# A two-layer graph attention kernel: fourteen edge tiles a layer fetched row by row, node rows kept in SBUF, a first stage with fixed row buffers

## The chip, the cores and the metric

The kernel runs on one core of a Trainium2 chip, as one program in one launch. The metric is the device time of one execution in microseconds (us), without a profiler. Before the change the median of three runs is 2140.39 us (2140.09 to 2140.89). One further execution was profiled, and all rows of profiles below come from such an execution.

The engines are named as in the profile: PE (TensorE; PEld is its weight load), DVE (VectorE), ACT (ScalarE), POOL (GpSimd) and SP (SyncE, which only issues transfers).

## What is computed

6250 nodes have 768 features each; 100,000 edges (src, dst) are sorted by dst, and each node has an edge to itself besides. Cut to what matters:

```python
h = maximum(layernorm(x), 0)                 # 6250 x 768
for W, heads in ((W1, 4), (W2, 1)):          # two layers
    h = h @ W                                # 256 features
    e = leaky_relu(alpha_s[src] + alpha_d[dst])
    w = exp(e - max over the edges of dst)
    h = sum over edges of dst (w * h[src]) / sum of w
    h = relu(h + b)
out = x + relu(h @ Wm1 + bm1) @ Wm2 + bm2
```

alpha_s and alpha_d are products of a node's 256 features with a vector for each head. The costly part is h[src]: 100,000 rows of about 1 KB a layer, at places that only the data tells.

## The kernel before, in words

Nodes are cut into 49 tiles of 128 (NT), edges into 784 tiles of 128 (NET). Tiles 2 to 783 hold edges, so a layer has 782. Four edge tiles are a group (196 groups, NG), two are a pair (392), and 16 belong to one node tile.

**First stage** (L236 to L375), one pass for each node tile. SP loads x and its transpose (L180, L245). DVE takes the moments (L251, L253), PE spreads the mean over partitions (L264), DVE subtracts it (L270), ACT applies relu (L272), and PE multiplies by W1, 12 matrix instructions (L281). ACT writes the result into `row`, one of 5 rotating buffers (L288), whose ones and scores POOL fills (L287, L306). POOL multiplies by the score vectors and halves the sum twice (L296, L299), DVE adds up the rest (L305). SP stores the row into `table1` in DRAM (L309). From tile 14 on one piece of `edge_places` (L186) is put between tiles: integer arithmetic on the edges' numbers by DVE, and their loads.

**The two edge stages** (`layer_edges`, L433). For every edge tile POOL issues one indirect transfer, which fetches 128 rows of the table at the places that a column of `src_i` holds (`gather`, L448, L456). It is issued 8 groups ahead (AHEAD), into 10 buffers. Six pairs a layer, `singles` (L122: pairs 71, 135, ... 391), are not fetched by POOL. SP fetches their 256 rows each, one transfer for a row (`fetch_singles`, L460). It loads 32 numbers of rows into registers (L465), and for each row computes the place and issues the transfer (L470). The generator is resumed once after each pair (L623, L636) and issues 4 rows, so that a pair takes 64 pairs' time and is there 7 pairs ahead of its use.

For each pair (`pair`, L532) ACT makes two exponentials of the sources' scores (L542, L544), DVE combines them with those of the destinations (L547) and scales the rows (layer 1, L559) or a one-hot matrix (layer 2, L554), and PE sums over edges by a one-hot product (L570). A group's sums run on in `acc` (L585). When a node tile is complete, `Node1.steps` adds the node's own row, divides, multiplies by W2 and stores into `table2` (L683 to L707). `Node2.steps` runs the two dense layers and stores the output (L775 to L817). The own row of a node comes from the table in DRAM: `prefetch` loads it from SP (L675, L760), and DVE uses it in `ahead` (L680) or `steps` (L778).

The order on each engine is the order in which the program is written (`manual_schedule`), so a waiting instruction holds up all behind it on its engine. SP has one queue, and on it stand the rows of `singles`, the own rows, the masks (L431, L493), destinations (L425), x and outputs. Every SP transfer counts on one of eight semaphores in turn, and waits for the one eight before it.

Of the kernel before, what the change touches and what calls it, by code (L numbers as in the profile page):

```python
# [11 lines left out]
BF16 = mybir.dt.bfloat16  # L12
I32 = mybir.dt.int32
AF = mybir.ActivationFunctionType
ALU = mybir.AluOpType
AX = mybir.AxisListType

P = 128
N = 6250
# [18 lines left out]
AHEAD = 8  # L38
SPAN = 8
ROWS = 4  # L40
REGS = 32
PAD_DST = 1 << 20
# [3 lines left out]
CH = P * TPC  # L46
NCH = EP // CH


@with_exitstack  # L50
def kernel(
# [68 lines left out]
    dcol = const.tile([P, NET], F32, name="dcol")  # L120

    singles = range(2 * TPG * SPAN + 7, NET // 2, 2 * TPG * SPAN)  # L122
    single_i = const.tile([1, len(singles), 2 * P], I32, name="single_i")
    dmod_d = dram.tile([NCH, CH], BF16, name="dmod_d")
# [58 lines left out]
    def heads_row(row):  # L183
        return row[:, :RW[1]].rearrange("p (h c) -> p h c", h=4)

    def edge_places(ones):  # L186

        dst_i = ones.tile([P, NET], I32, name="dst_i")
        dri = ones.tile([NCH, CH], I32, name="dri")
        for to, of in ((dst_i, dst_cols), (dri, dst_rows), (src_i, src_cols)):  # L190
            nc.sync.dma_start(to, of)
            yield
            yield
        nc.sync.dma_start(single_i, src_rows[singles[0]::singles.step].unsqueeze(0))
        yield
        for layer in bT:
            with nc.allow_non_contiguous_dma(reason="256 numbers"):
                nc.sync.dma_start(bT[layer], {1: b1, 2: b2}[layer].rearrange("(k p) -> p k", p=P))
            yield
        b = ones.tile([P, OUT_DIM // P], F32, name="b")  # L200
        with nc.allow_non_contiguous_dma(reason="768 numbers"):
            nc.sync.dma_start(b, bm2.rearrange("(p k) -> p k", p=P))
        yield

        drm = ones.tile([NCH, CH], BF16, name="drm")
        for d, n, w, to, f in ((dst_i, P, NET, dcol, dst_f), (dri, NCH, CH, drm, None)):
            m = ones.tile([n, w], I32, name=f"m{n}")
            nc.vector.tensor_scalar(m, d, P - 1, None, ALU.bitwise_and)
            yield
            if f is None:  # L210
                f = ones.tile([n, w], F32, name=f"f{n}")
            nc.vector.tensor_copy(f, d)
            yield
            far = ones.tile([n, w], F32, name=f"far{n}")
            nc.vector.tensor_scalar(far, f, float(N), 256.0, ALU.is_ge, ALU.mult)
            yield
            nc.vector.tensor_add(to, far, m)
            yield
        nc.sync.dma_start(dmod_d, drm)
        bp = ones.tile([P, 3, OUT_DIM // P], BF16, name="bp")  # L220
        rest = ones.tile([P, 2, OUT_DIM // P], F32, name="brest")
        in_parts(nc.vector, [bp[:, k] for k in range(3)], b, rest[:, 0], rest[:, 1])
        yield
        with nc.allow_non_contiguous_dma(reason="768 numbers"):
            nc.sync.dma_start(bm2_d.rearrange("s (p k) -> p s k", p=P), bp)
# [5 lines left out]
    rowsp = edges_stack.enter_context(tc.tile_pool(name="rows", bufs=3))  # L231
    maskp = edges_stack.enter_context(tc.tile_pool(name="masks", bufs=6))
    bm2_d = dram.tile([3, OUT_DIM], BF16, name="bm2_d")
    mask_d = dram.tile([NU * P, 8 * P], BF16, name="mask_d")
    edges_stack.enter_context(tc.manual_schedule())
    with tc.tile_pool(name="w1p", bufs=1) as wp, tc.tile_pool(name="x1", bufs=6) as xp, \  # L236
# [30 lines left out]
        def centre(i):  # L267
            m_ps, rstd = means.pop(i)
            c = wk.tile([P, KI, P], F32, name="cent")
            nc.vector.tensor_sub(c, xTs.pop(i), m_ps.unsqueeze(1).to_broadcast([P, KI, P]))  # L270
            r = wk.tile([P, KI, P], F32, name="r")
            nc.scalar.activation(r, c, AF.Relu)  # L272
            rs[i] = r, rstd
# [10 lines left out]
        def keep1(i, h_ps, rstd):  # L284
            row = wk.tile([P, TW[1]], F32, name="row", bufs=5)
            h = heads_row(row)[:, :, :HID // 4]
            nc.gpsimd.memset(heads_row(row)[:, :, HID // 4:], 1.0)  # L287
            nc.scalar.activation(h, h_ps.rearrange("p (h c) -> p h c", h=4), AF.Copy, scale=rstd)  # L288

            ha = wk.tile([P, 8, HID // 4], F32, name="ha")  # L290
            four = ha.rearrange("p (k h) c -> p k h c", k=2)
            of = h.unsqueeze(1).to_broadcast([P, 2, 4, HID // 4])
            if i == NT - 1:
                nc.vector.tensor_tensor(four, of, a1b, ALU.mult)
            else:
                nc.gpsimd.tensor_tensor(four, of, a1b, ALU.mult)  # L296
                for n in (HID // 8, HID // 16):
                    hb = wk.tile([P, 8, n], F32, name=f"ha{n}", bufs=4)
                    nc.gpsimd.tensor_tensor(hb, ha[:, :, :n], ha[:, :, n:], ALU.add)  # L299
                    ha = hb  # L300
            rows[i] = row, ha

        def scores1(i):
            row, ha = rows[i]
            nc.vector.tensor_reduce(sd[1][:, i], ha, AX.X, ALU.add)  # L305
            (nc.gpsimd if i < NT - 1 else nc.vector).tensor_copy(row[:, RW[1]:], sd[1][:, i, :4])  # L306

        def store1(i):
            nc.sync.dma_start(table[1][i * P:(i + 1) * P], rows.pop(i)[0])  # L309


        rows = {}
        warm_ps = ps.tile([P, 4 * P], F32, name="warm_ps", tag="o", bufs=3)
# [119 lines left out]
    def layer_edges(layer, H, node, pre, matched):  # L433
# [4 lines left out]
        with tc.tile_pool(name=f"eg{layer}", bufs=4) as eg, \  # L438
# [9 lines left out]
            def gather(g):  # L448
# [3 lines left out]
                for t in tiles(g):  # L452
                    k = TPG * g + t
                    if k // 2 in singles:
                        continue
                    nc.gpsimd.indirect_dma_start(  # L456
                        out=G[g][:, t], out_offset=None, in_=table[layer],
                        in_offset=bass.IndirectOffsetOnAxis(ap=src_i[:, k:k + 1], axis=0))

            def fetch_singles():  # L460

                for j, k in enumerate(singles):
                    single[k] = eg.tile([P, 2, TW[layer]], F32, name="single", bufs=2)
                    for r in range(0, 2 * P, REGS):
                        _, rows = nc.values_load_multi_w_load_instructions(  # L465
                            single_i[:, j, r:r + REGS], engines=(mybir.EngineType.SP,), min_val=0,
                            max_val=N - 1, skip_runtime_bounds_check_because="sources are nodes")
                        for i in range(REGS):
                            t, at = divmod(r + i, P)
                            nc.sync.dma_start(single[k][at:at + 1, t], table[layer][ds(rows[i], 1)])  # L470
                            if i % ROWS == ROWS - 1:
                                yield

            one_by_one = fetch_singles()


# [141 lines left out]
            for g in range(NG):  # L618
# [3 lines left out]
                advance(g)  # L622
                next(one_by_one, None)  # L623
                make_hot(g + 1)
# [10 lines left out]
                advance(g)  # L635
                next(one_by_one, None)  # L636
                if j == 3:
# [29 lines left out]
    with tc.tile_pool(name="w2p", bufs=1) as wp, tc.tile_pool(name="wk2", bufs=2) as wk:  # L667
        w2 = []

        class Node1:  # L670
            rows, mine = {}, {}

            def prefetch(self, t):
                self.rows[t] = wk.tile([P, RW[1]], F32, name="row1", bufs=3)
                nc.sync.dma_start(self.rows[t], table[1][t * P:(t + 1) * P, :RW[1]])  # L675

            def ahead(self, t):
                C = HID // 4
                self.mine[t] = wk.tile([P, 4, C + 1], F32, name="mine")
                nc.vector.tensor_mul(self.mine[t], heads_row(self.rows.pop(t)),  # L680
                                     pre1.own[:, t].unsqueeze(2).to_broadcast([P, 4, C + 1]))

            def steps(self, t, sum_):  # L683
# [17 lines left out]
                for _ in range(4):  # L701
                    yield 1
                row = wk.tile([P, TW[2]], F32, name="row2")
                nc.scalar.activation(row[:, :HID + 1], h_ps[:, :HID + 1], AF.Copy)
# [10 lines left out]
    with tc.tile_pool(name="wmp", bufs=1) as wp, tc.tile_pool(name="x3", bufs=4) as xp, \  # L715
# [39 lines left out]
        class Node2:  # L755
            rows, xs = {}, {}

            def prefetch(self, t):
                self.rows[t] = wk.tile([P, RW[2]], F32, name="row3", bufs=3)
                nc.sync.dma_start(self.rows[t], table[2][t * P:(t + 1) * P])  # L760
                for i in (t - 1, t) if t == NT - 1 else (t - 1,) if t else ():
# [13 lines left out]
            def steps(self, t, sum_):  # L775
                n = min(P, N - t * P)
                all_ = wk.tile([P, RW[2]], F32, name="all_")
                nc.vector.scalar_tensor_tensor(all_, self.rows.pop(t), pre2.own[:, t], sum_,  # L778
                                               ALU.mult, ALU.add)
# [340 lines left out]
```

## Time and profile before

| | us |
|---|---|
| median of three runs, without the profiler | 2140.39 |
| the profiled execution | 3330.35 |
| its span, first to last instruction | 3328.5 |
| first gather of layer 1 starts at | 160.26 |
| last gather of layer 1 starts at | 1817.05 |
| first gather of layer 2 starts at | 1881.18 |
| last gather of layer 2 starts at | 3266.36 |

In a group's row the columns are: line, engine, operation, tiles, count, then busy time and mean ns of one, then the engine's idle time before it and what ended it. "SPq" is SP's queue and "issue" is time in which the engine waited for nothing that the profile shows. Note the first two rows of the table: the profiled execution is 1190 us longer than one without the profiler.

### The profile page before, as it was taken

The numbers are of one execution on the slowest core, as the hardware profiler recorded it, in microseconds if no ns is written. First come the engines' busy times: TensorE is split into PE (matmuls) and PEld (weight loads), VectorE is DVE, ScalarE is ACT, GpSimd is POOL, SyncE is SP. The second block draws the span as 40 slices with busy tenths as digits, with TensorE's granted clock in tenths as the row PEclk, the third lists the DMA queues.
The fourth block names the chain that finished last, engine by engine and source line by source line (L and its number), as shares of the span: only waits on it lengthen the run. The fifth ranks groups of instructions, "written<-read, shape, count | busy, mean of one in ns | idle before, by whom it ended". The sixth has DMA issues, their size and how long they took to land. (4 is left out here: it accounts for less than half of the span.)

```text
span 3328.5 us, 35557 instructions
## 1 busy us (share of the span) xinstructions
PE 1634.9 (49%) x6633; PEld 1105.0 (33%) x6634; DVE 1401.5 (42%) x4321; ACT 554.9 (17%) x2549; POOL 1589.3 (48%) x1791
## 2 busy tenths in 40 slices
PE   9824434434344344344344535555555555564556
PEld 7612223222222222232222323433344333343334
DVE  7824434434344344344343524434443334343344
ACT  4501111111111111111111201111111111111112
POOL 7864434434434344344344255545554555554551
PEclk9956766767767667667776757777777767777768
DMA  9743333333333333333333334444444444444443
GB/s 343 256 132 103 102 98 100 103 95 101 99 98 101 95 104 103 95 100 100 99 101 92 92 96 121 125 121 130 122 121 122 126 124 127 122 126 117 118 128 99
DMA packets 176298, 395.60 MB, mean 119 GB/s; under 512 B 39757, under 2 KB 69674, under 8 KB 176066
## 3 DMA queue, kind: packets, MB, share of 16 engines
q0 software_dynamic: 73920, 205.89, 23.2%
q1 hardware_dynamic: 100908, 186.02, 16.7%
q10 hardware_dynamic: 1238, 1.32, 0.1%
q14 instruction: 175, 1.43, 0.1%
q8 instruction: 57, 0.93, 0.1%
HBM read 334.89 MB, written 58.19 MB: 118 GB/s over the span
## 5 line engine op out<-in xcount | busy, mean ns | idle before, releaser
L456 POOL DMA_INDIRECT G<-table,src_i x1540 | 1461.9, 949 | 1648.9 <-issue 1444.6
L570 PE MATMUL o_ps<-hw,hot 128*128 128x260 f32 x1564 | 610.3, 530 | 970.7 <-DVE hw L559 826.6
L570 PEld LDWEIGHTS o_ps<-hw,hot 128*128 128x128 f32 x1564 | 355.9, 252 | 1221.9 <-DVE hw L559 968.1
L570 PE MATMUL o_ps<-G,hw 128*128 128x258 f32 x1540 | 496.0, 468 | 56.6 <-issue 24.5
L547 DVE TENSOR_TENSOR e_ps<-e,e_ps 128x8 f32<-128x8 f32 (+1 forms) x782 | 127.9, 164 | 863.3 <-ACT e L544 400.3
L596 ACT ACTIVATE sum<-acc 32x260 f32<-32x260 f32 (+1 forms) x384 | 159.9, 416 | 1870.2 <-DVE acc L585 1237.0
L570 PEld LDWEIGHTS o_ps<-G,hw 128*128 128x128 f32 x1540 | 346.4, 237 | 155.8 <-issue 39.1
L680 DVE TENSOR_TENSOR mine<-row,own 128x260 f32<-128x260 f32 x49 | 21.0, 429 | 760.0 <-DMA row<-table 760.0
L554 DVE TENSOR_SCALAR hw<-iota_ps,dcol,w 128x128 f32<-128x128 f32 x782 | 284.8, 405 | 20.4 <-issue 3.1
L520 PE MATMUL e_ps<-win,mask 128*128 128x12 bf16 (+1 forms) x1564 | 62.8, 169 | 467.0 <-DMA mask<-mask_d 457.9
L559 DVE TENSOR_TENSOR hw<-G,e_ps 128x520 f32<-128x520 f32 x385 | 267.8, 696 | 21.9 <-issue 4.0
L807 PE MATMUL y_ps<-wm,mT 128*128 128x384 f32 x392 | 195.2, 631 | 96.4 <-ACT mT L798 91.2
L520 PEld LDWEIGHTS <-mask 128*128 128x128 bf16 x1564 | 60.4, 102 | 484.5 <-DMA mask<-mask_d 462.9
L585 DVE SCALAR_TENSOR_TENSOR acc<-acc,keep,o_ps 128x260 f32<-128x260 f32 (+1 forms) x388 | 184.5, 475 | 25.9 <-PE o_ps L570 15.7
L542 ACT ACTIVATE e<-G 128x8 f32<-128x8 f32 (+1 forms) x770 | 153.1, 199 | 80.4 <-issue 43.4
L544 ACT ACTIVATE e<-G 128x8 f32<-128x8 f32 (+1 forms) x770 | 147.9, 192 | 0.0
L281 PE MATMUL h_ps<-w,r 128*128 128x256 f32 x588 | 134.7, 382 | 6.6 <-ACT r L272 6.6
L807 PEld LDWEIGHTS y_ps<-wm,mT 128*128 128x128 f32 x392 | 82.6, 234 | 157.1 <-ACT mT L798 99.4
L502 DVE TENSOR_TENSOR hot<-iota_ps,dcol 128x512 f32<-128x512 f32 (+1 forms) x196 | 133.6, 682 | 0.0
L663 ACT ACTIVATE rT<-tp,bT 128x128 f32<-128x128 f32 x196 | 60.2, 357 | 381.2 <-PE tp L657 367.0
L281 PEld LDWEIGHTS h_ps<-w,r 128*128 128x128 f32 x588 | 107.9, 190 | 26.9 <-ACT r L272 11.5
L811 DVE TENSOR_TENSOR y<-y_ps,xt 128x384 f32<-128x384 f32 (+1 forms) x98 | 54.1, 552 | 91.6 <-PE y_ps L807 45.1
(403 smaller groups left out, 1165.6 us busy)
## 6 DMA issues: line engine op xcount, KB each, us to landing
xt<-in_x SPq DMA_DIRECT2D x96, 384.0 KB
drow<-dmod_d SPq DMA_DIRECT2D x49, 512.0 KB
mask_d<-mask SPq DMA_DIRECT2D x98, 256.0 KB
mask<-mask_d SPq DMA_DIRECT2D x98, 256.0 KB
G<-table,src_i POOLq DMA_INDIRECT x1540
single<-table SPq DMA_DIRECT2D x1536, 1.0 KB
single<-table SPq DMA_DIRECT2D x1536, 1.0 KB
xTt<-in_xT SPq DMA_DIRECT2D x49, 384.0 KB
```

Of the source, the lines that this page charges most:

```text
L281: nc.tensor.matmul(h_ps, r[:, k], w1[:, k], start=(k == 0), stop=(k == KI - 1))
L456: nc.gpsimd.indirect_dma_start(out=G[g][:, t], out_offset=None, in_=table[layer], in_offset=bass.IndirectOffsetOnAxis(ap=src_i[:, k:k + 1] ...
L502: nc.vector.tensor_tensor(hot[g][:, T[0]:T[0] + n], iota_ps.unsqueeze(1).to_broadcast([P, n, P]), dcol[:, k:k + n].unsqueeze(2).to_broadca ...
L542: nc.scalar.activation(e1, sc, AF.Exp)
L544: nc.scalar.activation(e2, sc, AF.Exp, scale=SLOPE)
L547: nc.vector.tensor_mul(v, e2, rho)
L554: nc.vector.tensor_scalar(hw[:, t], iota_ps, dcol[:, k:k + 1], w[:, t], ALU.is_equal, ALU.mult)
L559: nc.vector.tensor_mul(hw, Gp[:, :, :RW[1]].rearrange("p t (h c) -> p t h c", h=H), w.unsqueeze(3).to_broadcast([P, 2, H, C + 1]))
L570: nc.tensor.matmul(o_ps[g], l, r[:, :RW[layer]], start=(k == tiles(g)[0]), stop=(k == TPG - 1))
L585: nc.vector.scalar_tensor_tensor(acc, run[0], ones_c if last else keep[:, k:k + 1], o_ps.pop(g), ALU.mult, ALU.add)
L596: nc.scalar.activation(done[t][r], acc[r], AF.Copy)
L807: nc.tensor.matmul(y_ps, mT[:, j], wm2[:, j, s * half:(s + 1) * half], start=False, stop=(j == KH - 1))
```

## The change

Four things are changed.

1. **Pairs by rows.** Seven pairs a layer instead of six (59, 111, ... 371), five rows after each pair instead of four. A pair takes 52 pairs' time, and again is there 7 pairs ahead.
2. **Places in bytes.** In the first stage DVE multiplies the numbers of the sources by the row's size in bytes, for each layer (L231), and SP stores them into `place_d`. SP loads 256 of them for a pair, one pair ahead, and the number in the register is the place itself, the table being read as bytes.
3. **Own rows kept.** The 49 rows that the first stage makes stay in SBUF (`kept`, 1056 bytes a partition each). Layer 1 reads them there, `Node1.steps` writes its result over the same buffers and stores it to `table2` as before, and `Node2.steps` reads it there. The 98 loads at L675 and L760 are gone.
4. **First stage.** With a buffer for each tile the five rotating ones are gone. POOL writes the ones of all 49 ahead of the stage. The scores are copied into the row by ACT instead of POOL. In `edge_places` six of DVE's eight wide instructions go; ACT makes three wide conversions to float in their place. `cent`, `r`, `ha` have 2 buffers instead of 3, `ha32` 2 instead of 4.

```diff
+BY_ROWS = {"sync": (5, 32)}
+SLACK = 7
...
+    steps_ = -(-PAIR // rows_)
+    SINGLE[name_] = range(steps_ + SLACK, NET // 2, steps_)
...
-    singles = range(2 * TPG * SPAN + 7, NET // 2, 2 * TPG * SPAN)
...
-        for d, n, w, to, f in ((dst_i, P, NET, dcol, dst_f), (dri, NCH, CH, drm, None)):
-            m = ones.tile([n, w], I32, name=f"m{n}")
-            nc.vector.tensor_scalar(m, d, P - 1, None, ALU.bitwise_and)
-            nc.vector.tensor_copy(f, d)
-            nc.vector.tensor_scalar(far, f, float(N), 256.0, ALU.is_ge, ALU.mult)
-            nc.vector.tensor_add(to, far, m)
+        nc.scalar.activation(dst_f, dst_i, AF.Copy)
+        for d, to in ((dst_i, dcol), (dri, drm)):
+            nc.vector.tensor_scalar(d, d, PAD_DST | P - 1, None, ALU.bitwise_and)
+            nc.scalar.activation(to, d, AF.Copy)
...
+        for layer in (1, 2):
+            nc.vector.tensor_scalar(place, some, 4 * TW[layer], None, ALU.mult)
+            nc.sync.dma_start(place_d[layer], place)
...
+    kept = [keptp.tile([P, TW[1]], F32, name=f"kept{t}") for t in range(NT)]
...
-            row = wk.tile([P, TW[1]], F32, name="row", bufs=5)
-            nc.gpsimd.memset(heads_row(row)[:, :, HID // 4:], 1.0)
+            row = kept[i]
...
-            (nc.gpsimd if i < NT - 1 else nc.vector).tensor_copy(row[:, RW[1]:], sd[1][:, i, :4])
+            nc.scalar.activation(kept[i][:, RW[1]:], sd[1][:, i, :4], AF.Copy)
...
-                            nc.sync.dma_start(single[k][at:at + 1, t], table[layer][ds(rows[i], 1)])
-                            if i % ROWS == ROWS - 1:
+                of = table[layer].bitcast(U8).rearrange("n w -> (n w)").unsqueeze(0)
+                            eng.dma_start(to[p:p + 1, t * W:(t + 1) * W], of[:, ds(at[i], W)])
+                            if (r + i) % step == step - 1:
                                 yield
...
-                self.rows[t] = wk.tile([P, RW[1]], F32, name="row1", bufs=3)
-                nc.sync.dma_start(self.rows[t], table[1][t * P:(t + 1) * P, :RW[1]])
+                pass
...
-                row = wk.tile([P, TW[2]], F32, name="row2")
+                row = kept[t][:, :TW[2]]
...
-                self.rows[t] = wk.tile([P, RW[2]], F32, name="row3", bufs=3)
-                nc.sync.dma_start(self.rows[t], table[2][t * P:(t + 1) * P])
...
-                nc.vector.scalar_tensor_tensor(all_, self.rows.pop(t), pre2.own[:, t], sum_,
+                nc.vector.scalar_tensor_tensor(all_, kept[t][:, :RW[2]], pre2.own[:, t], sum_,
```

## The prediction, made before the result was known

> **What bounds the kernel now.** The first thing to read is a contradiction: the profiled execution took 3330.35 us (span 3328.5, and 1.85 around it), the median without the profiler is 2140.39. So 1190 us of this profile are not in the number to be predicted, and I first had to find which. I read, in this order, the groups by line of POOL, the list of waits, SP's timeline, then PE's timeline of the first stage.
>
> ```profile
> span 3328.5 us, 35557 instructions
> ...
> L456 POOL DMA_INDIRECT G<-table,src_i x1540 | 1461.9, 949 | 1648.9 <-issue 1444.6
> ```
>
> POOL has the most work in the edge stages, but waits longer than it works. Its timeline shows that this is two things:
>
> ```profile
> 1716.01 0.95 POOL L456 DMA_INDIRECT G<-table,src_i  x1 [0.30 <-issue]
> 1717.26 0.95 POOL L456 DMA_INDIRECT G<-table,src_i  x1 [0.30 <-issue]
> 1733.72 0.95 POOL L456 DMA_INDIRECT G<-table,src_i  x1 [15.51 <-issue]
> 1734.97 0.95 POOL L456 DMA_INDIRECT G<-table,src_i  x1 [0.30 <-issue]
> ```
>
> A gather costs POOL 1.25 us from start to start, 0.95 busy and a fixed 0.30; and about once for each node tile POOL stands for 15 us. Who makes it stand is in the waits:
>
> ```profile
> POOL G L456 <- issue: 1444.6, 1361, 17.4
> ...
> DVE mine L680 <- DMA row<-table: 760.0, 46, 17.9
> PEld L520 <- DMA mask<-mask_d: 462.9, 48, 22.3
> ```
>
> DVE waits once for each node tile of layer 1 for a row that SP has yet to request, PE in layer 2 for a mask; POOL then runs out of free buffers. SP's timeline tells why SP is late:
>
> ```profile
> 1130.64 3.50 SPq L470 DMA_DIRECT2D single<-table  x8
> 1134.24 0.36 SPq L493 DMA_DIRECT2D mask_d<-mask  x1
> 1134.79 21.74 SPq L470 DMA_DIRECT2D single<-table  x16
> ```
>
> The same instructions take 0.44 us a row in one line and 1.36 in the next. In the quick stretches a row takes 0.413 us (at 1016.04, four rows in 1.47 us: the last transfer's own 0.23 taken off, 1.24 over 3). I take the slow stretches to be made by the profiler, because without it there is no room for them:
>
> start to first gather 160.3; 770 gathers of 1.25 us, 962.5; layer change 14.8 (landing of the last gather 2.0, as from 1885.87 to its first use at 1887.87, less the fixed 0.3; from the last pairs' scores at 1868.05 to the next layer's first gather at 1881.18, 13.1); 962.5 again; end 21.8 (1.7 as before, one pair 1.1, and 19.0 from the last pair's scores at 3309.48 to the end); around the span 1.85. Sum 2123.8. The row buffer's memset at L705 stretches a gather by 0.12 us in each of 49 node tiles (1775.30 to 1776.67 is 1.37), 5.9 more: 2129.7. The median is 10.7 above that, 0.5%. So without the profiler POOL is in step for nearly all of the two edge stages: gathers times 1.25 us set the time, and SP, though busy, keeps up: per layer 1536 rows x 0.413 + 48 register loads x 2.14 (L465) + 49 x 1.85 for its other transfers = 828 us of POOL's 962.
>
> **The change, part by part** (against 2140.4; a difference under 0.2%, 4.3 us, cannot be told from none).
>
> 1. *Two more edge tiles a layer by rows.* POOL issues 768 gathers a layer instead of 770: 4 x 1.25 = **5.0 us** less, all on the path. SP gets 1792 rows a layer. The seven pairs end at 371, where the six ended at 391, the very last pair. So before, when the last gather had landed, pair 390 and then 391 were still to do; now only one. DVE needs 2.0 us from one to the other in layer 1 (1868.38 to 1870.42), of which 1.0 is a node's steps, and 1.0 in layer 2 (3303.51 to 3304.55): **2.0 us** together, between 0 and 3.
>
> 2. *Places in bytes.* A row on SP before is FUSED_REGOPS (37 ns), MOVE (29) and the transfer (228), 294 of 413 ns, so 40 ns between instructions. The built program has no register arithmetic on a row any more: 77 ns less, 0.336 us. Between two uses of the generator (one pair, 2.45 us of POOL) SP then has 5 x 0.336 = 1.68, a share of the register load 5/32 x 2.14 = 0.33, and its other transfers 1.43/8 = 0.18: 2.19 us, against 4 x 0.413 + 0.27 + 1.85/8 = 2.15 before. SP stays at 89% of POOL; in time, nothing. What is queued behind a late row is on SP the destinations, masks and outputs, and PE and DVE wait for these; POOL's cover is the 8 groups that it is ahead.
>  A rule speaks against this: the Trainium skill, "DMA: Bandwidth & Descriptors", section "Anatomy of one DMA", puts a fixed 2.0 us on each DMA. Paid one after another, 1792 rows would be 3584 us a layer. The row says otherwise: 0.413 us, since eight are under way at once; by the rule that leaves a floor of 2.0/8 = 0.25 us, below 0.336, and the list of SP's waits has only 24.7 us for rows waiting on rows. I go by the row; the rule decides if landing takes over 2.7 us. The new load of places (14 in all, one pair ahead) holds SP once for each layer, some 2 us at its start, where POOL's first gathers cover it.
>
> 3. *Own rows kept.* 98 transfers go, 0.42 and 0.36 us each on SP, counted above. In the profiled execution this takes away the 760 us wait at L680; in the median that wait has no room, as the sum shows, so **0**. At most the 10.7 us which the sum leaves open vanish with it. The DMA engines are at a share of 0.35 and 0.43 in the edge stages, so less traffic is worth nothing.
>
> 4. *First stage.* PE paces it: 2.70 us a node tile (products start at 126.70, 129.40, 132.10), POOL 2.65. But from 64.91 to 140.88, 25 tiles take 75.97 us where 67.5 would do: 8.5 us are lost.
>
> ```profile
> 67.50 0.27 PE L264 MATMUL mean_ps<-ident,mv 128*128 128x128 f32 x1
> 68.12 2.86 PE L281 MATMUL h_ps<-w,r 128*128 128x256 f32 x12 [0.35 <-ACT r L272]
> 70.82 0.27 PE L264 MATMUL mean_ps<-ident,mv 128*128 128x128 f32 x1
> 72.08 2.86 PE L281 MATMUL h_ps<-w,r 128*128 128x256 f32 x12 [0.99 <-ACT r L272]
> ...
> ACT row L288 <- DMA table<-row: 19.0, 14, 2.6
> ```
>
>  Here ACT waits for a row buffer to be stored, and its relu comes late. Near 68, 72 and 138 this costs 2.7 us, and fixed buffers end it. The other 5.7 lie between 83 and 113, beside the eight wide integer and float instructions of L208 to L217. The two at L208 stay (1.49 and 1.62 us; tiles late by 2.6). The rest, 3.1, can go. The Trainium skill, "SBUF — State Buffer", section "Who interferes with whom", has casts and tensor_scalar of DVE lock GpSimd out; by that rule the four of L212 and L215, 0.69 + 0.81 + 0.68 + 0.81, would give POOL back 3.0 us, and in the rows L299's two steps do swell there from 1.26 to 1.47 and 1.59. But PE sets the pace, not POOL, so I count PE's 3.1 and not POOL's 3.0 on top.
>  ACT gets three wide copies (nearest row: relu of 128x768, 0.84 us) and 49 small ones (L306, 0.19). ACT works 1.6 of 2.70 us, so the small ones are hidden by its idle time before L255 and L272 (0.35 and 0.45 a tile). A wide one overruns what is left, 0.6, and PE's lead of 0.3 hardly helps: up to 0.5 each, 1.5. The last tile's copy on ACT instead of DVE: 0.2. POOL's 49 memsets at the start (5.1 us at 0.104) lie in its idle stretch from 3.4 to 14.6. Fewer buffers: `r` of a tile is written when PE is through with the tile before the last, as PE is by then; 0. Bounds: 8.5 at best, 1.5 lost at worst (copies late, loads still full: the DMA share is 0.99 from 20 to 62 us). I take 2.7 + 3.1 - 1.7 = **4.1 us**.
>
> Sum: 5.0 + 2.0 + 4.1 = 11.1; 2140.4 - 11.1 = **2129.3 us**, 0.52% less.
>
> **The rivals.**
> - *First stage gains nothing* (0.17): the loads, at a share of 0.99, take over as the pace. For it: 337 GB/s are moved at full share from 62 to 83 us, and a tile's 922 KB in 2.70 us are 341. Against: the share is 0.90 and 0.92 later, so there is room to catch up. 2140.4 - 7.0 = 2133.4, to 2138 if the ends give nothing and the copies cost 1.5.
> - *SP becomes the bound, slower* (0.10). The profile never shows a row without FUSED_REGOPS; if the queue cannot take a transfer faster than every 0.413 us, or if rows read as bytes land later, a pair costs SP 2.06 + 0.33 + 0.18 = 2.57 us against 2.45. Over 364 pairs SP falls 44 us behind, less 7 pairs' lead (17): 27 us late in a layer; DVE at 2.29 us a pair (seven pairs from 1026.69 to 1042.75) regains 4 of it in the last 28 pairs, and in layer 2 more. About +35 - 11: 2164 us. It decides from 0.396 us a row.
> - *More hidden stalls go* (0.16): the 10.7 us that my sum leaves open are SP's, and the own rows' removal ends them: 2119. If the gather's 0.30 us gap is the profiler's too, more of the median was SP's, and it could be 2100.
>
> **How the numbers follow.** The forecast has 0.57 (2125 to 2134). The range of 2117 to 2139 holds it, the first rival and half of the third: 0.82. Faster by over 0.2% (below 2136.1): 0.57 + 0.16 + half of 0.17 = 0.81; within 0.2% 0.09; slower 0.10.
>
> **What would show it.** POOL: 1536 gathers, mean still 0.95, still 1.25 apart. SP: no FUSED_REGOPS at the rows, 0.33 to 0.35 us a row in the quick stretches. DVE's wait at the own rows gone. First gather at about 156. The profiled span itself must fall far more than the median: SP's instructions for a node tile go from about 105 to 88, which scales its 33.8 and 28.3 us a tile by 0.84, to 28.4 and 23.8, 49 x 9.9 = 485 us less, about 2840. I am wrong if gathers are not 1.25 apart without the profiler, if a row still takes 0.4 us, or if the first gather isn't earlier.

## The result, and the profile after

The changed kernel takes 2125.3 us (median of four executions, 2124.5 to 2126.7), the kernel before beside it 2140.2. The ratio is 0.9935, with a 95% interval of 0.9917 to 0.9952: 14.9 us less, where 11.1 had been forecast. Its profiled execution took 2126.68 us, so this profile runs at the pace of the median, as the one of before (3330.35) did not.

The page's first line, and its group of gathers (count, busy time, mean ns of one, idle time before them and what ended most of it):

```profile
span 2124.9 us, 33381 instructions
...
L473 POOL DMA_INDIRECT G<-table,src_i x1536 | 1463.3, 953 | 487.6 <-issue 347.2
```

Four gathers fewer, of the same 0.95 us. Their idle time is 0.32 us each, against more than 1 us before. POOL's timeline shows where the little that is left lies: the first gather, the last one of layer 1 and the first of layer 2 (start, duration, and in brackets the idle time before it):

```profile
154.08 1.13 POOL L473 DMA_INDIRECT G<-table,src_i  x1 [4.48 <-DMA table<-kept]
...
1119.14 0.95 POOL L473 DMA_INDIRECT G<-table,src_i  x1 [0.30 <-issue]
1135.58 0.95 POOL L473 DMA_INDIRECT G<-table,src_i  x1 [15.49 <-DVE win L423]
```

POOL stands still once, for 15.5 us, between the layers. From 154.08 to 1119.14 are 767 steps without a pause, 1.258 us each on average; the usual one is 1.25 (median 1.251). So the execution splits at POOL's gathers into five parts (for before no such split at the pace of its median exists):

| kernel | to first gather | layer 1 | layer change | layer 2 | after last gather | span |
|---|---|---|---|---|---|---|
| changed kernel | 154.1 | 965.1 | 16.4 | 963.9 | 25.4 | 2124.9 |

SP's timeline in the middle of layer 1 (xN are N transfers in a row) shows the rows and what stands between them:

```profile
603.89 8.97 SPq L503 DMA_DIRECT2D single_sync<-table  x20
612.96 0.36 SPq L527 DMA_DIRECT2D mask_d<-mask  x1
613.41 1.54 SPq L503 DMA_DIRECT2D single_sync<-table  x5
615.06 0.37 SPq L741 DMA_DIRECT2D table<-kept  x1
```

Five rows take 1.54 us; the last transfer's own 0.23 taken off, that is 0.328 us a row, and the median over all rows is 0.323. The stretch of 20 takes 2.5 us more than 19 such steps and a transfer, since a register load (2.12 us) lies in it.

In the first stage PE now starts a tile every 2.70 us, and the lists of waits of PE and PEld from 20 to 155 us have only these (total, times, longest):

```profile
PEld h_ps L298 <- ACT r L289: 3.0, 3, 1.8
PE h_ps L298 <- ACT r L289: 2.1, 2, 1.4
```

No wait of ACT for a row buffer's store is left.

### The profile page after: what moved, and what is told of

The parts are those of the page before. It is cut to its first block, busy times and chain, and to the rows that moved or that the text cites. A ratio compares the mean times of both kernels' runs of the same rounds, so it can differ in the third digit from the quotient of the medians.

```text
span 2124.9 us, 33381 instructions
## 1 busy us (share of the span) xinstructions
PE 1564.6 (74%) x6633; PEld 1047.7 (49%) x6634; DVE 1403.4 (66%) x4316; ACT 590.4 (28%) x2601; POOL 1581.6 (74%) x1739
## 3 DMA queue, kind: packets, MB, share of 16 engines
q1 hardware_dynamic: 87878, 173.59, 24.3%
q14 instruction: 157, 1.29, 0.2%
## 4 chain that ended last, share of the span: by engine, by line
DMA 28%; DVE 24%; POOL 15%; issue 12%; PE 11%; ACT 6%; SPq 3%; ACTq 0%; POOLq 0%; DVEq 0%
DMA G<-table,src_i 25%; POOL G L473 15%; DVE hw L593 7%; PE h_ps L298 5%; PE o_ps L604 3%; DVE acc L619 3%; DVE hw L588 3%; ACT sum L630 2%; ACT e L576 2%; DVE e_ps L581 2%; SPq L503 2%; PE y_ps L840 2%; DVE e_ps L591 2%; ACT e L578 1%; DVE hot L536 1%
## 5 line engine op out<-in xcount | busy, mean ns | idle before, releaser
L604 PE MATMUL o_ps<-hw,hot 128*128 128x260 f32 x1564 | 582.8, 511 | 283.7 <-DVE hw L593 220.7
L604 PE MATMUL o_ps<-G,hw 128*128 128x258 f32 x1536 | 475.7, 440 | 232.3 <-DVE hw L588 230.6
L604 PEld LDWEIGHTS o_ps<-hw,hot 128*128 128x128 f32 x1564 | 349.2, 245 | 486.0 <-DVE hw L593 350.6
L604 PEld LDWEIGHTS o_ps<-G,hw 128*128 128x128 f32 x1536 | 301.0, 213 | 374.9 <-DVE hw L588 325.4
L840 PE MATMUL y_ps<-wm,mT 128*128 128x384 f32 x392 | 186.6, 607 | 0.0
L591 DVE TENSOR_TENSOR e_ps<-e_ps,e 128x8 f32<-128x8 f32 x391 | 68.2, 174 | 13.4
L312 POOL TENSOR_TENSOR ha<-kept,a1b 128x512 f32<-128x512 f32 x48 | 56.8, 1183 | 23.2 <-ACT kept L304 23.0
L584 DVE TENSOR_TENSOR w<-e_ps,e 128x2 f32<-128x2 f32 x391 | 62.2, 159 | 13.3
L735 PE MATMUL h_ps<-w,rT 128*128 128x258 f32 x196 | 69.7, 493 | 0.5 <-ACT rT L699 0.5
```

The lines of the kernel that those rows point to most:

```text
L604: nc.tensor.matmul(o_ps[g], l, r[:, :RW[layer]], start=(k == tiles(g)[0]), stop=(k == TPG - 1))
L840: nc.tensor.matmul(y_ps, mT[:, j], wm2[:, j, s * half:(s + 1) * half], start=False, stop=(j == KH - 1))
```

## The experiments

Theory A is the prediction's: POOL's gathers and the two ends set the time, SP has a tenth of its time free. The rival: SP is the second limit, close behind. Twelve kernels ran in three groups of four, each group on one chip beside the kernel before. No kernel leaves out a part of the computation.

**c_after**, the changed kernel as it is.

> The changed kernel as it is, beside the others of this call on one chip: the measure for them. Theory A (POOL is in step for the whole of both edge stages, so the time is the first gather's start plus gathers times 1.257 us plus the ends): 2125, 0.993 of the kernel before. Theory B (part of the time was SP's, late with rows, own rows or masks): the same here; the two part in the runs beside it.

2124.25 us (2123.11 to 2125.39), 0.9927 [0.9914, 0.9941]; span 2122.4. This is what the next three are compared with.

**e1_twelve_tiles**

```diff
-BY_ROWS = {"sync": (5, 32)}
+BY_ROWS = {"sync": (4, 32)}
```

> Four rows after each pair instead of five, so six pairs a layer (71 to 391) as before the change; all else is the changed kernel. Theory A: four more gathers, 4 x 1.257 = 5.0 us, and the last pair is fetched ahead again, so that two are left to do behind the last gather, 2.0 us: 7.0 us slower than the changed kernel, 2132. Theory B: SP has a fifth fewer rows to issue, so nothing is lost: 2125 or below.

2133.0 us (2130.58 to 2134.58), 0.9964 [0.995, 0.9978]: 8.7 more than c_after. By the five parts (table below) the gathers take 6.2 more, which is four of them at 1.26 and a slightly slower pace, the layer change 3.1 and the end 2.2 more, the first stage 1.0 less. (These two traces lie 10.4 us apart, the medians 8.7.) Step 1 of the prediction holds, slightly larger than its 7.0.

What SP waited for while layer 1 was in full course tells how much of it was free. This is the list of SP's own waits from 240 to 1080 us, first of the changed kernel, then of e1:

```profile
SPq L503 <- DMA drow<-dmod_d: 45.4, 33, 2.6
SPq L527 <- DVE e_ps L591: 15.9, 25, 7.8
SPq L741 <- DVE kept L740: 13.5, 8, 4.2
SPq L527 <- DVE mask L525: 8.3, 1, 8.3
```

```profile
SPq L741 <- DVE kept L740: 88.9, 42, 4.0
SPq L527 <- DVE e_ps L591: 74.1, 37, 4.8
SPq L503 <- DMA drow<-dmod_d: 39.5, 26, 2.3
SPq L527 <- DVE e_ps L581: 14.8, 10, 3.5
SPq L527 <- DVE mask L525: 11.8, 9, 3.0
```

Waits for another engine are free time: SP stands there only because it is ahead. With four rows a pair they are 192 of 840 us (these lines and smaller ones), with five 46, or 5.5%. The first line of the changed kernel, with `drow`, is not free time. In all 33 cases it is the eighth transfer after a load of destinations that waits, the one that counts on the same semaphore: these loads landed 3.8 to 5.4 us after their issue, and eight rows take 2.6. That is 1.4 us each time. Waits for transfers are 67 us in all, so SP is at 95% in this stretch, not at 89%. While rows are still issued, up to 1055 us, it is closer still: 26 of 815 us are waits for engines, 3%.

**e2_place_by_registers**: the number of the source in the register and the place worked out from it, as before, with five rows a pair.

```diff
-            nc.vector.tensor_scalar(place, some, 4 * TW[layer], None, ALU.mult)
+            nc.vector.tensor_copy(place, some)
...
-                            eng.dma_start(to[p:p + 1, t * W:(t + 1) * W], of[:, ds(at[i], W)])
+                            eng.dma_start(single[k][p:p + 1, t], table[layer][ds(at[i], 1)])
```

> Seven pairs, five rows after each pair, but the register holds the number of the row and SP multiplies it, as before the change (one FUSED_REGOPS more for a row, 77 ns); the stored places are copies instead of products. Theory A: a row costs SP 0.32 + 0.08 = 0.40 us, a pair 2.0 + 0.33 + 0.18 = 2.51 us against POOL's 2.45; 364 x 0.06 = 22 us behind less 17 us of lead, so 5 us late at the end of a layer, 2125 to 2135. Theory B: the shorter row made most of the gain: 2138 or more. The profiled execution: about 15 instructions of rows for a pair against 12 before the change and 10 after; if the slow stretches of SP come from the profiler and from the rate of instructions, its span is far over 3000 us again while the time stays near 2130.

2271.9 us (2269.04 to 2273.58), 1.0618 [1.0604, 1.0633], 147 more than c_after. Theory A's 2125 to 2135 fell. SP's timeline and POOL's, in the same stretch of layer 1:

```profile
634.88 1.88 SPq L500 DMA_DIRECT2D single_sync<-table  x5
```

```profile
603.23 0.94 POOL L473 DMA_INDIRECT G<-table,src_i  x1 [0.30 <-issue]
613.32 0.94 POOL L473 DMA_INDIRECT G<-table,src_i  x1 [9.14 <-issue]
```

A row takes (1.88 - 0.23) / 4 = 0.413 us again, and POOL runs out of free buffers within the layer, four times in layer 1 and four times, for less, in layer 2. From 240 to 1080 us SP waits for other engines less than 10 us. SP is the bound. It also settles a second point: its profile is not stretched (span 2267.3), though SP issues more instructions for a pair than in the kernel before. The rate of SP's instructions under the profiler does not explain before's 3330 us.

**e3_own_rows_loaded**: the changed kernel, with a node tile's own row loaded from the table, and the results of layer 1 in rotating buffers, as before.

```diff
             def prefetch(self, t):
-                pass
+                self.rows[t] = wk.tile([P, RW[1]], F32, name="row1", bufs=3)
+                nc.sync.dma_start(self.rows[t], table[1][t * P:(t + 1) * P, :RW[1]])
...
-                row = kept[t][:, :TW[2]]
+                row = wk.tile([P, TW[2]], F32, name="row2")
...
```

The same loads come back in layer 2.

> The changed kernel, but both layers load the own rows from the tables by SP again (98 transfers). Theory A: SP's load rises by 0.05 us a pair to 2.2 of 2.45, nobody waits: 2125, within 1 us of the changed kernel. Theory B: the own rows came late and their wait is part of the gain: 2130 to 2136. Profiled span within 10 us of the time, if the rate of instructions decides (10.9 a pair).

2144.3 us (2138.29 to 2150.72 over 21 executions), 1.002 [1.0012, 1.0028]: 20 more than c_after, where theory A had 0. POOL's gathers are as quick as before; the time is lost in one place, at the layer change:

```profile
1151.15 0.94 POOL L473 DMA_INDIRECT G<-table,src_i  x1 [30.46 <-DVE win L423]
```

30.5 us where the changed kernel has 15.5. SP's waits of e3 from 240 to 1080 us say why:

```profile
SPq L503 <- DMA drow<-dmod_d: 56.3, 38, 2.7
SPq L503 <- DMA row<-table: 5.3, 11, 1.3
...
SPq L503 <- DMA table<-row: 4.5, 10, 0.8
```

Waits for other engines are down to 9 us in all, none of them among these lines: one more load for each node tile, its 0.42 us and the waits behind it, has used up SP's last 5%. SP's last row of layer 1 goes out at 1083.8 us instead of 1055.3, the last result of layer 1 at 1147.8 instead of 1132.3, and the first gather of layer 2 starts 3.3 us after that in both. DVE stands at the own rows again (whole execution),

```profile
DVE mine L716 <- DMA row<-table: 88.1, 43, 4.0
```

a wait that the changed kernel doesn't have. So the work behind the gathers falls back. In c_after ACT starts on a pair's scores 3 to 7 us after the start of the pair's last gather, all through layer 1; in e3 it is 11 us at first and 22 to 25 towards the end. POOL doesn't stand for it, because it is 8 groups ahead, 40 us of gathers; it pays for the lag when the next layer has to wait for the last result. That the loads cost this, and not the rotating result buffers that e3 brings back with them, is read from these waits; the two were not run apart.

The five parts of all these executions, from the starts of the first and last gathers in each trace:

| kernel | to first gather | layer 1 | layer change | layer 2 | after last gather | span |
|---|---|---|---|---|---|---|
| c_after | 153.9 | 966.0 | 15.8 | 962.4 | 24.3 | 2122.4 |
| e1, four rows | 152.9 | 969.7 | 18.9 | 964.9 | 26.5 | 2132.8 |
| e3, own rows loaded | 152.4 | 967.4 | 31.4 | 962.3 | 24.4 | 2137.9 |
| e4, and rotating buffers | 154.7 | 966.9 | 30.6 | 963.2 | 25.4 | 2140.8 |
| e5, and numbers on DVE | 157.7 | 967.5 | 29.9 | 961.4 | 25.0 | 2141.5 |
| e2, places by registers | 152.8 | 1015.6 | 65.9 | 983.8 | 49.2 | 2267.3 |
| e6, six rows | 152.6 | 1042.9 | 44.9 | 1012.3 | 36.1 | 2288.8 |

The traces of e3, e4 and e5 are of quick executions of each (2139.6, 2142.8 and 2143.3 us, where the medians are 2144.3, 2148.8 and 2151.2); what makes the others longer is not shown.

**e4_rotating_rows**: e3 with five rotating row buffers in the first stage, as before.

```diff
-            row = kept[i]
+            row = kept[i] = wk.tile([P, TW[1]], F32, name="row", bufs=5)
+            nc.gpsimd.memset(heads_row(row)[:, :, HID // 4:], 1.0)
...
-            nc.scalar.activation(kept[i][:, RW[1]:], sd[1][:, i, :4], AF.Copy)
+            (nc.gpsimd if i < NT - 1 else nc.vector).tensor_copy(kept[i][:, RW[1]:], sd[1][:, i, :4])
```

> As the run with own rows loaded, and the first stage uses five rotating row buffers again, with POOL's memset and score copy in each tile; conversions of edge numbers stay on ACT. Theory A with the split of the prediction (row buffers 2.7 us, edge numbers 3.1 less 1.5): 3 us slower than that run, about 2128. The other split, that the stage's losses come from DVE's and POOL's work on the edge numbers alone: no difference. A third, that the buffers were nearly all of it: 6 us, 2131.

2148.8 us (2142.24 to 2153.9), 1.0042 [1.0025, 1.0059]: 4.5 more than e3, with wide ranges on both sides. The first gather starts 2.3 us later than in e3, but ten executions with the changed first stage have it anywhere from 152.4 to 154.1, so this is rough too. ACT waits for a row's store again:

```profile
ACT row L304 <- DMA table<-row: 10.6, 8, 2.2
```

**e5_numbers_on_dve**: e4 with the eight wide instructions of `edge_places` on DVE, as before. What is left of the change is the fourteen tiles, the places in bytes and the smaller numbers of `cent`, `r` and `ha` buffers.

```diff
-        nc.scalar.activation(dst_f, dst_i, AF.Copy)
...
-        for d, to in ((dst_i, dcol), (dri, drm)):
-            nc.vector.tensor_scalar(d, d, PAD_DST | P - 1, None, ALU.bitwise_and)
...
-            nc.scalar.activation(to, d, AF.Copy)
+        for d, n, w, to, f in ((dst_i, P, NET, dcol, dst_f), (dri, NCH, CH, drm, None)):
+            m = ones.tile([n, w], I32, name=f"m{n}")
+            nc.vector.tensor_scalar(m, d, P - 1, None, ALU.bitwise_and)
...
+            nc.vector.tensor_scalar(far, f, float(N), 256.0, ALU.is_ge, ALU.mult)
...
+            nc.vector.tensor_add(to, far, m)
```

> As the run with rotating rows, and the edge numbers are converted by eight wide DVE instructions again instead of two on DVE and three on ACT. What is left of the change is 14 tiles a layer with places in bytes. Split of the prediction: 1.6 us slower than with rotating rows (3.1 given back, 1.5 for ACT saved), about 2130; if the numbers were nearly all of the stage's loss, 5 us, 2131 to 2133. Together with the run before it: 2140.2 less 5.0 and 2.0 for the tiles should be left, 2133.

2151.2 us (2143.31 to 2154.91), 1.0054 [1.004, 1.0068]: 2.4 more than e4, the first gather 3.0 later. And the fourteen tiles by rows with places in bytes, alone, are 11 us slower than the kernel before, where theory A had 2133. They put SP at its limit, and nothing relieves it: from 240 to 1080 us its waits for other engines are 10 us.

**e6_six_rows**: `BY_ROWS = {"sync": (6, 32)}`, sixteen edge tiles a layer.

> The changed kernel with six rows after each pair: eight pairs a layer, 1532 gathers. A pair costs SP 6 x 0.323 + 0.40 + 0.18 = 2.52 us against 2.45 of POOL. Theory A: 5.0 us less from the gathers, and SP falls 0.07 us a pair behind, 24 us over 344 pairs less 17 us of lead, some 7 us late in a layer and then regained by DVE in the 48 pairs left: 2120 to 2126. Rival: SP over POOL's pace holds up masks and outputs for the whole layer, +25 us a layer: 2165 or more.

2294.3 us (2290.63 to 2297.68), 1.0726 [1.0711, 1.074]. The rival was right in kind, and too low with 2165: at 0.323 us a row, six rows are too many, as five were at 0.413. POOL stands within the layer again, for 13.1 us before its gather at 546.79.

**e7_act_rows_too**: a second queue takes rows, two a pair on ACT.

```diff
-BY_ROWS = {"sync": (5, 32)}
+BY_ROWS = {"sync": (5, 32), "scalar": (2, 32)}
```

> The changed kernel, and ACT's queue fetches three more pairs a layer (135, 263, 391) by two rows after each pair, so 20 tiles a layer by rows, 1524 gathers; one tile of the check of the data is computed in place to make room. Theory A: 12 gathers less, 15.1 us, and the last pair is fetched ahead, which costs 2.0 at the ends: 2112. Rival: ACT stands 2.1 us for each load of 32 registers and 0.3 us for a row in front of the exponentials that all later work waits for; ACT is busy 0.28, but where the consumer has 0.16 us of room a pair in layer 1, 0.6 + 0.13 us a pair of ACT make it the bound: 2150 or more.

2703.3 us (2699.66 to 2709.32), 1.2632 [1.2611, 1.2652]. Theory A fell; the rival said "2150 or more", and it is 550 more. Its longest waits:

```profile
ACT sum L630 <- DVE acc L619: 1026.2, 356, 15.4
DVE e_ps L581 <- ACT e L578: 955.5, 476, 26.3
POOL G L473 <- issue: 858.0, 1230, 26.7
```

The first of these tells little, since it is 1046.4 us in e3 too. The second does: 590.6 us in c_after, at most 4.2 at a time, against 26.3 here. Rows on ACT stand in one queue with the exponentials that DVE waits for. How much of the 579 us over c_after (another chip) is this, and how much the masks that PE waits for (543.5 us), was not taken apart.

For the last four the theory was restated, as theory C: SP, with its waits for transfers, is the second limit, at 95% of POOL's pace. They ran on a third chip, and there every execution took about half as long again, nine others of the kernel before among them (median 3314.17, 3306 to 3325). The changed kernel itself did not run there. They are compared only with each other.

**c_before**, the kernel before as it is.

> The kernel before once more, for a second profile. Theory C (SyncE is the second limit: in the changed kernel it is at about 95% of GpSimd's pace, and the stretched profile of the kernel before belonged to that one execution): a span near 2138, no stretched rows, a GpSimd pause at the layer change of 20 to 30 us, longer than the 16.4 of the changed kernel, since SyncE loads the own rows too and is the later engine at the end of layer 1. Rival (the profiler always stretches this kernel's SyncE): a span above 3000 again.

3315.74 us, span 3314.0: theory C fell on all three of its numbers. The rival named the span rightly, but not its cause, since other executions on this chip were as long. The page's first line, a wait, and SP's timeline:

```profile
span 3314.0 us, 35557 instructions
```

```profile
POOL G L456 <- issue: 1429.7, 1355, 16.4
```

```profile
599.84 1.77 SPq L470 DMA_DIRECT2D single<-table  x4
601.72 0.35 SPq L493 DMA_DIRECT2D mask_d<-mask  x1
602.26 24.05 SPq L470 DMA_DIRECT2D single<-table  x16
```

This looks like the profile that the prediction was made from: quick rows, then sixteen in 24 us. The stretched pace belongs to the chip, or to its condition at that time: all 23 executions of this group took 3156 us or more, while the profiled ones of c_after, e1 and e3 took 2124 to 2140. So it needs neither the profiler nor an accident of one execution. TensorE's granted clock is lower in this group, 0.70 to 0.72 against 0.81 to 0.87 in the others without e7, but e7, at 0.75, has no such stretches either. Which chip the first profile came from is not on record.

**e10_twelve_by_registers**: e2 with `BY_ROWS = {"sync": (4, 32)}`.

> Twelve tiles, the place worked out by register arithmetic, own rows kept: e2 with four rows a pair in place of five. Theory C: a pair's share on SyncE is 4 x 0.413 + 8 x 2.14 / 64 + 0.2 + 0.13 for waits = 2.25 of GpSimd's 2.46 us, so GpSimd stays the bound: 2133 to 2137, against 2133.0 with twelve tiles by bytes. Rival (register arithmetic itself upsets SyncE, whatever the number of rows): above 2150.

3224.3 us, 0.9738 [0.9708, 0.9768] of the kernel before on this chip.

**e8_eight_pairs**

```diff
-BY_ROWS = {"sync": (5, 32)}
+BY_ROWS = {"sync": (48, 32)}
...
-    steps_ = -(-PAIR // rows_)
+    steps_ = rows_
...
-                            if (r + i) % step == step - 1:
+                            if (r + i + 1) * step % PAIR < step:
                                 yield
-                    yield
```

> Sixteen edge tiles a layer by rows: 256 rows spread evenly over 48 pairs (5, 5, 6 rows) in place of five a pair over 52. Theory C: SyncE has 2.41 of GpSimd's 2.46 us a pair, 98%, over the whole layer: four gathers fewer are worth 5.0, and the layer change loses about as much: 2119 to 2130. Rival (SyncE is already over GpSimd's pace at five rows): above 2135.

3163.7 us, 0.9558 [0.9525, 0.9592]. SP's timeline has the quick and the slow rows of this chip here too, with nothing but moves and transfers between them:

```profile
607.36 25.52 SPq L503 DMA_DIRECT2D single_sync<-table  x22
...
641.20 1.53 SPq L503 DMA_DIRECT2D single_sync<-table  x5
```

**e9_eight_pairs_act**: e8 with `drow` at L442 and the masks at L448 loaded by `nc.scalar`.

> e8 with the loads of the destination rows and of the second layer's masks issued by ScalarE. Theory C: SyncE loses 0.06 us of issue and 0.13 of waits a pair, 2.22 of 2.46 us or 90%: GpSimd is the bound and four gathers fewer give 2119 to 2121, the fastest version. Rival (ScalarE's own work is held up behind these loads, as it was by its rows in e7): above 2130.

3379.0 us, 1.0189 [1.0164, 1.0214], the slowest of the four.

On this chip SP has these slow stretches in every version, so none of these three tells what it would do at 2120 us, and none of their expectations was decided. Whether sixteen tiles can be had by relieving SP stays open; among the kernels measured at the quicker pace the changed one is the fastest. Why SP is slower here isn't settled. In the slow stretches its instructions start 0.70 us apart, or two or three times that, moves and transfers alike. The Trainium skill, "Runtime: NRT & Kernel Launch", section "Instruction fetch mechanics", says that each engine streams its instructions in through a DMA queue and that this is mostly hidden. The traces do not show the fetch late: packets of the instruction queues take 0.42 to 0.44 us here (8 KB, median) against 0.31 to 0.38 in the two other groups, and 1.0 to 1.1 us (16 KB) in all three. By that section a block of 16 KB holds 256 instructions, so a late one would be expected to make one long pause and not 0.70 us at each instruction.

## Why the prediction was right in size, and where it was wrong

The median fell by 14.9 us where 11.1 was forecast, inside the range. Undone one after the other, the parts look different from the forecast, each number being the difference of two medians (e3 and e4 ran on different chips, and e3 to e5 vary by some 10 us, so 2 us either way means nothing):

| part | forecast | measured | from |
|---|---|---|---|
| fourteen tiles and places in bytes | -7.0 | +11.2 | e5 against before |
| edge numbers on ACT | -3.1, and +1.5 for ACT's copies | -2.4 | e4 against e5 |
| fixed row buffers | -2.7, and +0.2 | -4.5 | e3 against e4 |
| own rows kept | 0 | -20.1 | c_after against e3 |
| sum | -11.1 | -15.8 | against before: 14.9 in the first result |

In this order two differences of about 20 us, with opposite signs and one cause, cancel. In another order they don't arise. e1 has everything but the two tiles and is 6.5 us below before on its chip. The first stage is 4.3 of that (step 4), which leaves 2.2, not clear of noise, for the places in bytes and the own rows together, where the forecast had 0; the two tiles then give 8.7, where it had 7.0. So the sum is not mere luck. What the forecast missed is that the tiles pay only once the own rows are gone; that the room which SP had left was enough, 5% where 11% were counted, was luck in part.

*Step 1, two more tiles.* Right once SP has room: 8.7 for 7.0, by e1. The layer change and the end gave 5.3 in the traces, beyond the 0 to 3 that step 1 allowed. Why is open; TensorE's granted clock was 0.82 in e1 and 0.85 in c_after, and whether that is part of it is not shown.

*Step 2, places in bytes.* The size of a row was right: 0.336 us said, 0.323 measured. The step that failed is "SP stays at 89% of POOL; in time, nothing". Its count of instructions stands: of the 840 us from 240 to 1080, 46 are waits for engines and 67 are waits for transfers, which leaves 727, or 87%. It left out these 67 us, 45 of them for loads of destinations, 8% of SP's time. It took only the first of these two lines from SP's list of waits before; a row that waits for a load of destinations stands in the second, under the load's name:

```profile
SPq L470 <- DMA single<-table: 24.7, 41, 1.4
...
SPq L470 <- DMA drow<-dmod_d: 12.7, 33, 0.6
```

The prediction had even named the sign, a landing over 2.7 us (eight rows at 0.336), but looked for it at rows only. Its 2.0 us was no measure of it either: the Trainium skill, "DMA: Bandwidth & Descriptors", section "Anatomy of one DMA", gives that for transfers on GpSimd's path, not on SP's, and the loads of destinations took 3.8 to 5.4. With the waits SP is at 95% in the changed kernel, and at its limit with one more load a node tile.

*Step 3, own rows.* The "0" failed with it. With twelve tiles it may stand, as the 2.2 above says; with fourteen the wait at the own rows has room at this pace too: e3 has 88 us of it and is 20 us slower. The 98 transfers were counted at SP's issue time and found affordable; without them SP gets from no room to some 5%. The two parts are one: the rows by bytes need the room that the own rows' removal makes.

*Step 4, first stage.* Right in mechanism and nearly in size. On the third chip the first gather starts at 157.1 us in c_before and at 152.8 in all three kernels with the changed first stage: 4.3 us, for a forecast of 4.1. Undoing both edits moves it from 152.4 in e3 to 157.7 in e5, 5.3 us. What ACT's copies cost was not measured alone. POOL's halvings are held up by DVE as the prediction said, 60.3 us in e5 (L321) against 57.3 in e4 (L315), but the 3.0 us agree by luck: the four casts and comparisons that it counted add 1.1 us, and two additions (L223 in e5) that it did not count add 1.5.

*The sum.* No trace of before at this pace tells what the 10.7 us left open were. In the changed kernel, where POOL does not stand within a layer, the prediction's terms are too short in three places as well, so they need not have been SP's stalls. Steps of gathers over 1.29 us, 43 in layer 1, add 5.8 us, and 25 in layer 2 add 5.0; the prediction had 5.9 in layer 1 and nothing in layer 2. The layer change takes 16.4 us where 14.8 less 1.0 was expected, the end 25.4 where 21.8 less 1.0 was. The 5.9 was also put down to the wrong instruction: the 47 steps of layer 1 before beside the memset at L705 average 1.25 us, while 45 of the 49 long ones lie beside DVE's `hot` (L502), as the one at 1775.30 does.

*The rivals.* SP as the bound did not come in the changed kernel, but its mechanism is real: e2 has it at 0.413 us a row. Its price was too low, 2164 for a measured 2272: in e2's trace the rows of layer 1 take 1004 us for 364 pairs, 2.76 us a pair instead of 2.57, and waits for transfers are part of it. Put at 8% of a pair, 0.20 us, they move the point from which SP decides from 0.39 us a row by the prediction's terms (it said 0.396) to (2.45 - 0.33 - 0.18 - 0.20) / 5 = 0.35, an estimate. The kernel is 0.03 us a row away from it.

*The signs.* The gathers, the rows without register arithmetic, the missing wait at the own rows and the earlier first gather came as said. The span of "about 2840" did not come: 2124.9. The step "I take the slow stretches to be made by the profiler" failed: on the third chip every execution is slow and all four traces show them, while on the other chips profiled executions have none. What followed from it for the median, that they have no room there, was right all the same.

## What to carry to other kernels

A queue's load is its issue time plus the waits of its instructions for transfers. Take these from the list of that queue's own waits, under every transfer's name, and count as free only what it waits for other engines. With a fixed number of semaphores in turn, one large transfer holds up the small one that shares its semaphore. When several parts of a change use one engine that is near its limit, they can't be priced one by one: here the rows alone lose 11 us, and the four parts together gain 15. An engine that runs ahead through a ring of buffers hides the lag of the one behind it until the end of the stage, so look for the cost at the stage change and not where it arises.

## What the runs showed of the hardware that was not expected

- The same kernel takes 2140 us on the chips of two groups and 3314 on that of a third. On it SP's rows, 0.4 us apart in some stretches, come 1.5 us apart in others, and the cause is open.
- A register load of 32 values takes SP 2.13 us. The changed kernel has 56 of them in a layer: 119 of 965 us, 12% of SP's time.
- A load of 512 KB (`drow`) lands 3.8 to 5.4 us after its issue where it was waited for, and the eighth transfer after it, on the same semaphore, waits 1.4 us on SP (45.4 us in 33 times); a count of the queue's instructions doesn't show this.
- Rows on ACT's queue, two for each pair, cost 579 us (e7 against c_after, on two chips), and DVE's waits for ACT's exponentials grow from 590.6 to 955.5 us.
- Beside two additions of DVE, on 784 and 1024 numbers a partition, POOL's halving takes 0.61 and 0.86 us longer than usual in e5; beside casts and comparisons of the same sizes only 0.20 to 0.33.
